# Attention scores of two key heads as two 64-row tiles of the matmul array instead of 96 or 100 zero-padded rows

## The chip, the cores and the metric

The kernel runs on one core of a Trainium2 chip. The metric is device time in microseconds (us) of one execution; the time before is the median of three executions. One further execution was recorded by the hardware profiler, and every duration below comes from it. Engine names are those of the profile: PE is the matmul array, PEld its weight loads, DVE the vector engine, ACT the scalar engine, POOL the general engine, SP the queue from which this kernel issues its DMAs.

## The reference, cut to what matters

Two layers run one after the other on `x` of 2 x 512 tokens x 512 channels, each with a modulated layer norm, an attention block and a feed-forward block. Layer 0 is a gated chunked linear attention with 32 heads of 128, then a ternary-weight feed-forward. Layer 1 is a softmax attention with small heads (which the change touches), then a mixer of four streams whose 4x4 matrices are balanced by 50 Sinkhorn iterations per token.

```python
# layer 1 attention: 32 query heads, 8 key heads, 16 channels each; called with x of 2 x 512 x 512
xq = (x @ wq + bq).reshape(B, S, H, D)
xk = (x @ wk + bk).reshape(B, S, KV, D)
xv = (x @ wv + bv).reshape(B, S, KV, D)
q = _rope(xq, cos, sin)
k = _rope(xk, cos, sin)
k = jnp.repeat(k, REP, axis=2)          # REP = 4 query heads per key head
v = jnp.repeat(xv, REP, axis=2)
scores = jnp.einsum('bqhd,bkhd->bhqk', q, k) / jnp.sqrt(jnp.float32(D))
probs = jax.nn.softmax(scores.astype(jnp.float32), axis=-1)
out = jnp.einsum('bhqk,bkhd->bqhd', probs, v).reshape(B, S, E)
```

## The kernel before, in words

**Number format of the scores.** A score is a sum over 16 channels, which the kernel computes with 48 rows of the array: queries and keys are each split into a high and a low part, the queries stand in memory as (high, high, low) and the keys as (high, low, high), 3 x 16 = 48 rows per key head (`q_dram`, `k_dram`, written by `rope_halves`, L665). The exponent needs the row's maximum subtracted, and that too is done by the matmul: two further rows hold the negated maximum, again as a high and a low part, against key rows that are one.

**A step and its tiles.** A step (`order`, L1185) is one batch `b`, one half of the 512 queries (256) and one of four pairs `t` of key heads; there are 16. For a step, `key_rows` and `keys1` (L786, L793) fill two tiles `ks`, one for each key head s of the pair, [128, 512]: head 0 has its keys in rows 0 to 47 and zeros in 48 to 95, head 1 zeros in 0 to 47 and its keys in rows 48 to 95, and rows 96 to 99 hold the ones and zeros that pick the right maxima. `queries1` (L800) fills two tiles `qs`, one for each pair `rp` of query heads, [128, 2, 256], with the queries of head 0 in rows 0 to 47 and of head 1 in rows 48 to 95. So every score matmul contracts 96 rows (`KS`) for the maxima or 100 (`KM`) for the weights, of which 48 or 50 bring something. The zeros come from constants (`c_keys1`) that `layer1_keys` (L741) loads, copies on ACT and spreads by DMA over six tiles `ks`; three sets of key tiles rotate over the steps (`key_tile`).

**Pieces.** A step is worked in eight pieces, so there are 128. Piece k of a step does in `maxima` (L834) two score matmuls of 512 columns (L843), 128 queries against 512 keys, and a DVE maximum over each (L847). After each fourth piece the eight columns of maxima are split into high and low parts (L853, L854), transposed on PE (L857), copied by ACT (L862) and sent by a DMA into rows 96 to 99 of `qs` (L863). `weigh` (L865) does for a piece four score matmuls of 256 columns with the operands swapped (keys stationary, L877), and ACT takes the exponential of two at a time (L68, tile `pt`). After four pieces (a quad) `outputs` (L887) multiplies by the values: 32 matmuls in column tiles of 32 (L897), then ACT copies (L909), and `finish` (L911) transposes (L918), divides and adds to the residual.

**Order.** A loop over 64 units of layer 0 issues the first pieces from unit 53 on (`FIRST`, `PER`, `HOLD`), so layer 1's attention for batch 0 runs beside layer 0's end for batch 1; the rest follows in the loop of `piece` (L1219), which calls `maxima`, then, 10 pieces behind (`LAG`), `weigh`, then `outputs` and `finish`, and steps the generators `streams` (the mixer) by two steps per piece (`aside`). The tile framework orders the instructions within each engine's queue from its own estimate of their times, with the priorities and order-only dependencies (`anchor`, `behind`, L897's "one run of column tiles") that the kernel adds. PSUM tiles `s1` (L842) and `s2` (L874) are asked for with three buffers each (`S1`, `S2`). After the last piece the last two mixer groups finish alone.

Of the kernel before, what the change touches and what calls it, by code (L numbers as in the profile page):

```python
# [9 lines left out]
FP = mybir.dt.float32  # L10
FR = mybir.dt.float32r
W1 = 2
PT, OUT = 16, 1
S1, S2, MT, OT, OP = 3, 3, 2, 2, 2
# [18 lines left out]
AF = mybir.ActivationFunctionType  # L33
ALU = mybir.AluOpType
AX = mybir.AxisListType
PSUM = bass.MemoryType.PSUM

P = 128
B, L, HID = 2, 512, 512
NC = L // P  # L40
# [13 lines left out]
def tile_adaln(ctx: ExitStack, tc: tile.TileContext, a: dict, out: bass.AP):  # L54
    nc = tc.nc
# [6 lines left out]
    psp = ctx.enter_context(tc.tile_pool(name="ps", bufs=2, space=PSUM))  # L62
# [4 lines left out]
    def act(o, i, func, **kw):  # L67
        ins = nc.scalar.activation(o, i, func, **kw)  # L68
        tc.add_manual_dep(
            ins.ins, table.ins.name,  # L70
            mybir.DependencyInfo(mybir.DependencyClass.NoSync, mybir.DependencyReason.DATA),
            reason="the activation table",
        )
        return ins.ins
# [43 lines left out]
    anchor = {}  # L118
# [33 lines left out]
    def temp(shape, dt, name, bufs=2):  # L152
        return wk.tile(shape, dt, name=name, bufs=bufs)

    def bank(shape, name, bufs=2):
        return psp.tile(shape, FP, name=name, bufs=bufs)
# [42 lines left out]
    def raw_tile(load):  # L199
        raw = raws.tile([P, KC * P], FP, name="raw")  # L200
        nc.sync.dma_start(out=raw, in_=load)
        return raw
# [153 lines left out]
    ps = bank([64, HID], "mps")  # L356
# [285 lines left out]
    k_dram = [dram.tile([KV1, 48, L], FP, name=f"k_dram{b}") for b in range(B)]  # L642
# [88 lines left out]

    Q = L // 2
    NQ = Q // P
    KS, KM = 96, 100
    ksd = {}

    holder = {}

    def layer1_keys(js=(0, 1)):  # L741
        for s in range(2):
            empty = temp([P, L], FR, "hi1")
            nc.scalar.copy(empty, raw_tile(a["c_keys1"][s]))
            for j in js:
                ksd[j, s] = temp([P, L], FR, f"ks{j}{s}")
                nc.sync.dma_start(out=ksd[j, s].bitcast(FP), in_=empty.bitcast(FP))

    steps = [(g, b) for g in range(KV0 - AHEAD) for b in range(B)]
    steps += [(g, b) for b in range(B) for g in range(KV0 - AHEAD, KV0)]  # L750
# [33 lines left out]
    def key_tile(i):  # L784
        return i % 2 if i < TWO else (i - TWO + 2) % 3

    def key_rows(i):
        j = key_tile(i)
        if j == 2 and (2, 0) not in ksd:
            layer1_keys((2,))  # L790
        return [ksd[j, s] for s in range(2)]

    def keys1(i):  # L793
        b, t = order[i]["b"], order[i]["t"]
        order[i]["ks"] = key_rows(i)
        holder[key_tile(i)] = i
        for s in range(2):
            nc.sync.dma_start(out=order[i]["ks"][s].bitcast(FP)[48 * s:48 * s + 48], in_=k_dram[b][2 * t + s])

    def queries1(i):  # L800

        b, half, t = (order[i][n] for n in ("b", "half", "t"))
        assert l1c["there", b]
        pair = []
        for rp in range(2):
            qs = temp([P, 2, Q], FR, "qs", QS)
            for s in range(2):
                h = 8 * t + 4 * s + 2 * rp
                nc.sync.dma_start(
                    out=qs.bitcast(FP)[48 * s:48 * s + 48],  # L810
                    in_=q_dram[b][h:h + 2, :, half * Q:half * Q + Q].rearrange("r k q -> k r q"),
                )
            pair.append(qs)
        return pair
# [18 lines left out]

    def maxima(st, k):  # L834

        assert holder[key_tile(st["i"])] == st["i"]
        rp, j = divmod(k, 4)
        s, i = divmod(j, 2)
        if j == 0:
            st["m"] = small.tile([P, NQ * 2, 2], FP, name="m")  # L840
        for qt in range(NQ):
            ps = psp.tile([P, L], FP, name="s1", bufs=S1)  # L842
            anchor["pe"] = nc.tensor.matmul(  # L843
                ps, lhsT=st["qs"][rp][0:KS, i, qt * P:(qt + 1) * P], rhs=st["ks"][s][0:KS],
                start=True, stop=True,
            ).ins
            anchor["dve"] = nc.vector.tensor_reduce(  # L847
                st["m"][:, 2 * qt + s, i:i + 1], ps, AX.X, ALU.max, negate=True
            ).ins
        if j == 3:  # L850
            m2 = small.tile([P, NQ * 2, 2, 2], FR, name="m2")
            hi, lo = m2[:, :, 0], m2[:, :, 1]
            nc.vector.tensor_copy(hi, st["m"])  # L853
            nc.vector.tensor_tensor(lo, st["m"], hi.bitcast(FP), ALU.subtract)  # L854
            mt = psp.tile([8, Q], FP, name="mt", bufs=MT)
            for qt in range(NQ):
                nc.tensor.transpose(  # L857
                    mt[:, qt * P:(qt + 1) * P],
                    m2[:, 2 * qt:2 * qt + 2].bitcast(FP).rearrange("p a b c -> p (a b c)"), ident,
                )  # L860
            mm = temp([8, L], FR, "mm")[:, 0:Q]
            nc.scalar.copy(mm, mt)  # L862
            anchor["sp"] = nc.sync.dma_start(out=st["qs"][rp].bitcast(FP)[96:100], in_=mm.bitcast(FP)).ins  # L863

    def weigh(st, k):  # L865

        assert holder[key_tile(st["i"])] == st["i"]
        rp, r = divmod(k, 4)
        kp, s = divmod(r, 2)
        if r == 0:  # L870
            quads.append({"st": st, "rp": rp, "pt": {}})
        qd = quads[-1]
        for i in range(2):
            ps = psp.tile([P, 2, Q], FP, name="s2", bufs=S2)  # L874
            for j in range(2):
                kt = 2 * kp + j
                nc.tensor.matmul(  # L877
                    ps[:, j, :], lhsT=st["ks"][s][0:KM, kt * P:(kt + 1) * P], rhs=st["qs"][rp][0:KM, i, :],
                    start=True, stop=True,
                )  # L880
            p = wts.tile([P, 2, Q], FP, name="pt", bufs=PT)
            anchor["act"] = qd["last"] = act(p, ps, AF.Exp, scale=0.25)
            qd["pt"][2 * s + i, kp] = p

    quads = []

    def outputs(j):  # L887


        qd = quads[j]  # L890
        st = qd["st"]
        op = psp.tile([P, 2, Q], FP, name="op", bufs=OP)[:, 0, :]
        first = None
        with tc.high_priority(UPO):
            for kt in range(NC):
                for r in (3, 0, 1, 2):
                    mm = nc.tensor.matmul(  # L897
                        op[32 * r:32 * r + 32, :], lhsT=va[st["b"]][kt // 2][:, kt % 2, 2 * st["t"] + r // 2, :],
                        rhs=qd["pt"][r, kt // 2][:, kt % 2, :], start=kt == 0, stop=kt == NC - 1,
                    ).ins  # L900
                    if first is None:
                        first = mm
                        last_pt = qd["last"]
                        for m in (anchor["pe"], last_pt):
                            tc.add_manual_dep(mm, m.name, order_only, reason="behind the scores at hand")
                    else:
                        tc.add_manual_dep(mm, first.name, order_only, reason="one run of column tiles")
        qd["os"] = temp([P, L], FP, "os")[:, 0:Q]
        nc.scalar.copy(qd["os"], op)  # L909
# [57 lines left out]
    def streams(b, c0, n, last, ways):  # L967
# [217 lines left out]
    order = [  # L1185
        {"b": b, "half": half, "t": t} for b in range(B) for half in range(2) for t in range(4)
    ]
# [11 lines left out]
    def load_step(i):  # L1199
        if i < len(order):  # L1200
            o = order[i]
            o["i"] = i
            o["qs"] = queries1(i)
# [4 lines left out]
    def begin():  # L1208
        with behind():
            row_tiles(0, (GA,))  # L1210
        load_step(0)
        keys1(0)
        values1(0)
# [5 lines left out]
    def piece():  # L1219
        p = at[0]  # L1220
        at[0] += 1
        if p == 0:
            begin()
        i, k = divmod(p, 8)
        if k == 0 and i < len(order):
            load_step(i + 1)
        if p < n_pieces:
            maxima(order[i], k)
        if wt[0] <= p - slack(p):
            weighed()  # L1230
        if k == 4 and i + 1 < len(order):
            keys1(i + 1)
        with tc.high_priority(UP):
            if p >= HOLD and p % POP == 0 and virtual:
                tail(virtual.pop(0))
        aside(2)
# [64 lines left out]
    for n, u in enumerate(units):  # L1301
        g, b, c = u["at"]
        s = n // NC
# [127 lines left out]
```

## Time and profile before

| | |
|---|---|
| median of 3 executions | 1407.75 us (1398.83 to 1408.99) |
| the profiled execution: its own time | 1409.56 us |
| its span, first to last instruction | 1407.8 us |
| mean granted clock of PE | 0.944 |
| busy: PE, DVE, ACT, POOL | 1247.3, 1164.4, 825.1, 787.2 us |
| L843, the maxima's score matmuls | 256, first at 898.3 us, last at 1261.4 us |
| L877, the weights' score matmuls | 512, from 925.1 to 1275.6 us |
| L847, DVE maxima | 256, mean 673 ns |
| L68 on `pt`, ACT exponentials | 256, mean 601 ns |
| last matmul of layer 0's projections (L233) | ends at 1116.6 us |

How to read it: the busy time of an engine is the union of its instructions' records. A matmul's record is longer than the time for which it holds the array, since the next one starts before its end; what it holds is read from the distance of two starts. A wait is put down to the instruction that came last. The granted clock of PE is the share of its full clock, recorded in steps of about 3.41 us, each at 1.0 or at 0.5.

### The profile page before, as it was taken

To read this page: it belongs to the slowest core of one execution; us is meant where nothing else is said; L and a number is where in the kernel's file an instruction comes from. 1 tells how busy PE (TensorE), PEld (TensorE's weight loads), DVE (VectorE), ACT (ScalarE), POOL (GpSimd) and SP (SyncE) were. 2 spreads that over 40 slices of the span, in tenths; PEclk is the share of its full clock that TensorE was granted. 3 is DMA by queue.
4 is the path that set the end of the run, shared out by engine and by line. 5 is a ranking of instruction groups with operands and counts; after the bars stand their busy time and mean duration, and the time that the engine had idled before them with its cause. 6 is when DMAs were issued, how large, how long until landed. Compare 5 with 4: busy or idle time off the path is not lost. (4 is left out here: it accounts for less than half of the span.)

```text
span 1407.8 us, 23038 instructions
## 1 busy us (share of the span) xinstructions
PE 1247.3 (89%) x7128; PEld 990.5 (70%) x7128; DVE 1164.4 (83%) x3171; ACT 825.1 (59%) x2333; POOL 787.2 (56%) x1180
## 2 busy tenths in 40 slices
PE   6979999999999999999988998899998899994117
PEld 3767888788788778888876777677776667762116
DVE  7998668687677687787999977788699879888998
ACT  5456576476476466666665655567567467653226
POOL 4363274365264367577777757644243644657854
PEclk9999999999999999999999999999999899986568
DMA  7121241231131233224333327623212331100001
GB/s 241 36 70 43 87 124 39 68 106 53 53 118 56 94 117 111 81 79 128 120 106 90 98 70 233 179 66 97 65 42 94 101 92 48 59 2 1 1 15 46
DMA packets 95378, 117.14 MB, mean 83 GB/s; under 512 B 10828, under 2 KB 50508, under 8 KB 95256
## 3 DMA queue, kind: packets, MB, share of 16 engines
q1 hardware_dynamic: 95256, 115.67, 27.6%
q8 instruction: 57, 0.93, 0.3%
q14 instruction: 65, 0.53, 0.1%
HBM read 102.11 MB, written 10.64 MB: 80 GB/s over the span
## 5 line engine op out<-in xcount | busy, mean ns | idle before, releaser
L847 DVE TENSOR_REDUCE m<-s 128x1 f32<-128x512 f32 x256 | 166.6, 673 | 21.8 <-PE s L843 21.5
L68 ACT ACTIVATE pt<-s 128x512 f32<-128x512 f32 x256 | 137.4, 601 | 33.1 <-PE s L877 31.5
L448 POOL TENSOR_TENSOR q<-xcos,rot 128x512 f32<-128x512 f32 x64 | 92.8, 1450 | 56.5 <-DVE xcos L446 52.5
L68 ACT ACTIVATE sg<-sg 128x512 f32<-128x512 f32 x128 | 80.7, 632 | 64.5 <-DVE sg L479 62.5
L496 POOL TENSOR_SCALAR_AFFINE_SELECT dec<-gb 128x512 f32<-128x512 f32 x64 | 48.3, 755 | 121.2 <-DMA gb<-g_dram 65.4
L843 PE MATMUL s<-ks,qs 96*128 96x512 f32 x256 | 104.9, 442 | 11.5 <-DVE m L847 7.6
L877 PE MATMUL s<-qs,ks 100*128 100x256 f32 x512 | 104.4, 309 | 10.2 <-DMA qs<-mm 6.8
L233 PE MATMUL pps<-hh,wq_h 128*128 128x512 f32 x256 | 103.3, 403 | 7.1 <-ACT vT L767 3.4
L877 PEld LDWEIGHTS s<-qs,ks 100*128 100x128 f32 x512 | 82.7, 199 | 32.8 <-issue 7.9
L68 ACT ACTIVATE dec<-dec,room 128x128 f32<-128x128 f32 x256 | 83.0, 398 | 34.8 <-POOL dec L496 34.6
L233 PE MATMUL ops<-wo_h,zh 128*128 128x512 f32 x256 | 102.2, 399 | 1.2 <-ACT zh L571 1.0
L233 PE MATMUL gps<-wg_h,hh 128*128 128x512 f32 x256 | 101.3, 398 | 1.5 <-ACT wg_h L210 1.2
L233 PE MATMUL ops<-wo_h,zl 128*128 128x512 f32 x256 | 101.5, 396 | 0.7 <-DVE zl L572 0.7
L233 PE MATMUL pps<-hl,wq_h 128*128 128x512 f32 x256 | 101.8, 398 | 0.0
L233 PE MATMUL pps<-hh,wq_l 128*128 128x512 f32 x256 | 101.5, 397 | 0.0
L233 PE MATMUL gps<-wg_l,hh 128*128 128x512 f32 x256 | 101.1, 395 | 0.0
L233 PE MATMUL ops<-wo_l,zh 128*128 128x512 f32 x256 | 100.6, 393 | 0.0
L233 PE MATMUL gps<-wg_h,hl 128*128 128x512 f32 x256 | 100.6, 393 | 0.0
L516 POOL TENSOR_TENSOR gb<-gb,q 128x512 f32<-128x512 f32 x48 | 62.3, 1299 | 60.3 <-ACT gb L68 46.7
L549 PE MATMUL yps<-v,dec 128*128 128x128 f32 x512 | 93.4, 278 | 2.7 <-DVE xcos L446 1.4
L555 ACT ACTIVATE z<-yps 128x128 f32<-128x128 f32 x256 | 67.5, 278 | 41.1 <-PE yps L551 30.5
L559 DVE SCALAR_TENSOR_TENSOR z<-yps,ss,sg 128x128 f32<-128x128 f32 x256 | 72.0, 340 | 22.5 <-ACT ss L68 22.3
(321 smaller groups left out, 3984.4 us busy)
## 6 DMA issues: line engine op xcount, KB each, us to landing
gb<-g_dram SPq DMA_DIRECT2D x64, 256.0 KB
raw<-in_wq SPq DMA_DIRECT2D x56, 256.0 KB
raw<-in_wg SPq DMA_DIRECT2D x48, 256.0 KB
raw<-in_wo SPq DMA_DIRECT2D x48, 256.0 KB
raw<-in_wmod SPq DMA_DIRECT2D x40, 256.0 KB
qs<-q_dram SPq DMA_DIRECT2D x64, 96.0 KB
q_dram<-hi SPq DMA_DIRECT2D x16, 256.0 KB
raw<-in_wk SPq DMA_DIRECT2D x14, 256.0 KB
```

The lines of the kernel that those rows point to most:

```text
L68: ins = nc.scalar.activation(o, i, func, **kw)
L233: nc.tensor.matmul(ps, lhsT=l, rhs=r, start=i == 0, stop=i == n - 1)
L448: nc.gpsimd.tensor_tensor(dst, sp(xc_), sp(rot), ALU.add)
L496: anchor["pool"] = nc.gpsimd.affine_select(out=dec, in_=gb, pattern=[[0, REP0], [1, P]], compare_op=ALU.is_ge, fill=-1e30, base=0, channel ...
L516: nc.gpsimd.tensor_tensor(gb, gb, q[:, c], ALU.mult)
L549: nc.tensor.matmul(yps[:, h, :], lhsT=u["pr"][:, h, :], rhs=u["v"][:, c, :], start=True, stop=not c)
L555: nc.scalar.activation(z[:, h, :], yps[:, h, :], AF.Square, accum_out=ss[:, h:h + 1])
L559: nc.vector.scalar_tensor_tensor(z[:, h, :], yps[:, h, :], ss[:, h:h + 1], sg[:, h * P:(h + 1) * P], ALU.mult, ALU.mult)
L843: anchor["pe"] = nc.tensor.matmul(ps, lhsT=st["qs"][rp][0:KS, i, qt * P:(qt + 1) * P], rhs=st["ks"][s][0:KS], start=True, stop=True,).ins
L847: anchor["dve"] = nc.vector.tensor_reduce(st["m"][:, 2 * qt + s, i:i + 1], ps, AX.X, ALU.max, negate=True).ins
L877: nc.tensor.matmul(ps[:, j, :], lhsT=st["ks"][s][0:KM, kt * P:(kt + 1) * P], rhs=st["qs"][rp][0:KM, i, :], start=True, stop=True,)
```

## The change

Each key head's scores become a matmul of their own 48 rows (`KS`) or 50 (`KM`), head 0 on rows 0 to 63 of the array and head 1 on rows 64 to 127. One tile `ks` then holds both heads of a step, so there are three in place of six, and only two rows of ones per head are set up, by small DMAs from one loaded constant. The two matmuls of a pair, s = 0 and s = 1, are issued one right after the other, into two PSUM tiles that are both taken before the first of them. A piece of `maxima` is now one 128-query tile of both heads in place of two tiles of one; a piece of `weigh` is 128 keys of both heads with the 512 columns of both query heads in one matmul, in place of two matmuls of 256 for each head. The DMA of the maxima becomes two, one for each head.

```diff
-    KS, KM = 96, 100
+    KS, KM = 48, 50
...
     def layer1_keys(js=(0, 1)):
-        for s in range(2):
-            empty = temp([P, L], FR, "hi1")
-            nc.scalar.copy(empty, raw_tile(a["c_keys1"][s]))
-            for j in js:
-                ksd[j, s] = temp([P, L], FR, f"ks{j}{s}")
-                nc.sync.dma_start(out=ksd[j, s].bitcast(FP), in_=empty.bitcast(FP))
+        empty = temp([P, L], FR, "hi1")
+        nc.scalar.copy(empty, raw_tile(a["c_keys1"][0]))
+        for j in js:
+            ksd[j] = temp([P, L], FR, f"ks{j}")
+            for s in range(2):
+                nc.sync.dma_start(
+                    out=ksd[j].bitcast(FP)[64 * s + KS:64 * s + KM], in_=empty.bitcast(FP)[96:98]
+                )
...
-            nc.sync.dma_start(out=order[i]["ks"][s].bitcast(FP)[48 * s:48 * s + 48], in_=k_dram[b][2 * t + s])
+            nc.sync.dma_start(out=order[i]["ks"].bitcast(FP)[64 * s:64 * s + KS], in_=k_dram[b][2 * t + s])
...
-                    out=qs.bitcast(FP)[48 * s:48 * s + 48],
+                    out=qs.bitcast(FP)[64 * s:64 * s + KS],
...
         rp, j = divmod(k, 4)
-        s, i = divmod(j, 2)
+        i, qt = divmod(j, 2)
         if j == 0:
             st["m"] = small.tile([P, NQ * 2, 2], FP, name="m")
-        for qt in range(NQ):
-            ps = psp.tile([P, L], FP, name="s1", bufs=S1)
+        pss = [psp.tile([P, L], FP, name="s1", bufs=S1) for s in range(2)]
+        for s in range(2):
             anchor["pe"] = nc.tensor.matmul(
-                ps, lhsT=st["qs"][rp][0:KS, i, qt * P:(qt + 1) * P], rhs=st["ks"][s][0:KS],
-                start=True, stop=True,
+                pss[s], lhsT=st["qs"][rp][64 * s:64 * s + KS, i, qt * P:(qt + 1) * P],
+                rhs=st["ks"][64 * s:64 * s + KS], start=True, stop=True,
             ).ins
+        for s in range(2):
             anchor["dve"] = nc.vector.tensor_reduce(
-                st["m"][:, 2 * qt + s, i:i + 1], ps, AX.X, ALU.max, negate=True
+                st["m"][:, 2 * qt + s, i:i + 1], pss[s], AX.X, ALU.max, negate=True
             ).ins
...
-            anchor["sp"] = nc.sync.dma_start(out=st["qs"][rp].bitcast(FP)[96:100], in_=mm.bitcast(FP)).ins
+            for s in range(2):
+                anchor["sp"] = nc.sync.dma_start(
+                    out=st["qs"][rp].bitcast(FP)[64 * s + KS:64 * s + KM], in_=mm.bitcast(FP)[4 * s:4 * s + 4]
+                ).ins
...
-        for i in range(2):
-            ps = psp.tile([P, 2, Q], FP, name="s2", bufs=S2)
-            for j in range(2):
-                kt = 2 * kp + j
-                nc.tensor.matmul(
-                    ps[:, j, :], lhsT=st["ks"][s][0:KM, kt * P:(kt + 1) * P], rhs=st["qs"][rp][0:KM, i, :],
-                    start=True, stop=True,
-                )
+        pss = [psp.tile([P, 2, Q], FP, name="s2", bufs=S2) for s in range(2)]
+        for s in range(2):
+            nc.tensor.matmul(
+                pss[s], lhsT=st["ks"][64 * s:64 * s + KM, kt * P:(kt + 1) * P], rhs=st["qs"][rp][64 * s:64 * s + KM],
+                start=True, stop=True,
+            )
+        for s in range(2):
             p = wts.tile([P, 2, Q], FP, name="pt", bufs=PT)
-            anchor["act"] = qd["last"] = act(p, ps, AF.Exp, scale=0.25)
-            qd["pt"][2 * s + i, kp] = p
+            anchor["act"] = qd["last"] = act(p, pss[s], AF.Exp, scale=0.25)
+            qd["pt"][s, kt] = p
...
-                        rhs=qd["pt"][r, kt // 2][:, kt % 2, :], start=kt == 0, stop=kt == NC - 1,
+                        rhs=qd["pt"][r // 2, kt][:, r % 2, :], start=kt == 0, stop=kt == NC - 1,
```

## The prediction, made before the changed kernel ran

> **What bounds the kernel now.** First the page: busy shares and the granted clock of PE in 40 slices.
>
> ```profile
> PE 1247.3 (89%) x7128; PEld 990.5 (70%) x7128; DVE 1164.4 (83%) x3171; ACT 825.1 (59%) x2333; POOL 787.2 (56%) x1180
> ...
> PEclk9999999999999999999999999999999899986568
> ```
>
> The changed matmuls run from 898 to 1276 us, so the second view is the windows of that part: PE, PEld, DVE, ACT, POOL busy, then clock, DMA share, GB/s.
>
> ```profile
> 895.00:1000.00 105.00, 96.89 (x558) 76.86 (x557) 90.35 (x189) 69.68 (x192) 48.45 (x43) 0.97 0.33 92
> 1000.00:1135.00 135.00, 125.70 (x889) 93.68 (x887) 124.48 (x323) 83.81 (x220) 62.37 (x86) 0.95 0.25 79
> 1135.00:1280.00 145.00, 135.07 (x1163) 94.33 (x1163) 119.22 (x445) 95.90 (x230) 79.83 (x316) 0.93 0.14 40
> 1280.00:1408.00 128.00, 42.27 (x258) 40.00 (x258) 115.87 (x759) 43.55 (x156) 84.15 (x318) 0.63 0.05 17
> ```
>
> PE leads, DVE is close behind; after 1280 only the mixer's DVE and POOL work is left, which the change doesn't touch. I call 895 to 1135 the mixed stage (layer 0 still runs) and 1135 to 1280 the attention stage. Third, the groups and the waits of the attention stage.
>
> ```profile
> L847 DVE TENSOR_REDUCE m<-s 128x1 f32<-128x512 f32 x124 | 81.4, 673 | 18.9 <-PE s L843 18.7
> L68 ACT ACTIVATE pt<-s 128x512 f32<-128x512 f32 x144 | 76.2, 600 | 20.5 <-PE s L877 19.8
> L877 PE MATMUL s<-qs,ks 100*128 100x256 f32 x288 | 58.6, 310 | 7.5 <-DMA qs<-mm 6.8 <-ACT pt L68 0.6
> L843 PE MATMUL s<-ks,qs 96*128 96x512 f32 x123 | 50.3, 436 | 1.2 <-DVE m L847 1.2
> ...
> L897 PE MATMUL op<-pt,va 128*32 128x256 f32 x608 | 42.4, 423 | 0.5 <-ACT pt L68 0.5
> ```
>
> ```profile
> ACT os L909 <- PE op L897: 25.4, 17, 3.2
> ...
> DVE m L847 <- PE s L843: 18.7, 19, 3.1
> ...
> PE s L877 <- DMA qs<-mm: 6.8, 8, 2.1
> ```
>
> The others wait for PE; DVE could give back 18.7 us at most. Fourth, PE's timeline, since records overlap and only starts tell what a matmul holds.
>
> ```profile
> 1164.80 0.40 PE L843 MATMUL s<-ks,qs 96*128 96x512 f32 x1
> 1165.04 0.40 PE L877 MATMUL s<-qs,ks 100*128 100x256 f32 x2
> ...
> 1166.67 0.39 PE L843 MATMUL s<-ks,qs 96*128 96x512 f32 x1
> 1166.99 1.94 PE L897 MATMUL op<-pt,va 128*32 128x256 f32 x32
> 1168.86 0.50 PE L843 MATMUL s<-ks,qs 96*128 96x512 f32 x1
> ```
>
> 512 columns hold PE 0.237 us, 256 half of it. Into the column tiles it is 0.32 (0.09 more), and out of them about as much: 0.31 from the last start of `op`. One `op` of 32 matmuls takes 1.87 us by the chain of waits, and 3.45 where the clock is halved (1136.7). Last, the clock, by windows of its own 3.41 us steps; here I show the busy time of all engines, clock last but two.
>
> ```profile
> 1201.67:1205.08 3.41, 2.48 (x15) 1.72 (x14) 3.29 (x9) 1.24 (x4) 1.27 (x6) 1.00 0.22 60
> ...
> 1235.80:1239.22 3.42, 3.42 (x14) 2.74 (x12) 2.96 (x10) 3.07 (x9) 2.10 (x8) 0.50 0.00 0
> 1239.22:1242.63 3.41, 3.41 (x33) 1.39 (x32) 1.38 (x8) 0.57 (x2) 1.78 (x9) 0.50 0.00 0
> ...
> 1252.87:1256.28 3.41, 2.76 (x14) 1.79 (x13) 3.41 (x13) 1.84 (x5) 1.31 (x6) 1.00 0.01 2
> ```
>
> The step after 1252.87 is at half, though PE was busy 2.76 us; the one after 1201.67 stays full with 2.48; 1235.80 is all busy, with scores, and the next is still at half. What orders these is columns weighted by rows: counting each matmul's columns times its share of 128 rows (384 for a maxima matmul, 200 for a weight one, 512 for each four of `op`, whose plain float32 takes two passes), by start times, the steps hold 3,130 (stays full), 3,050 (stays half) and 2,900 (falls). I take 3,090 as the bound. It falls in 5 of the 42 steps of the attention stage.
>
> **The change, part by part.** *Key tiles.* Three loads of 256 KB, three ACT copies of 618 ns and ten DMAs of 256 KB go; ten DMAs of 4 KB come. They lie at 842 to 890, beside a DMA share of 0.77 (850 to 900); ACT waits there 10.7 us for weights (`wg_h`), PE only 1.2 for ACT. I take -1, bounds -4 and 0.
>
> *Scores, mixed stage.* 133 maxima matmuls and 224 weight ones start there: 133 x 0.237 + 224 x 0.118 = 58 us of PE. In full pairs half goes, 29. Two row tiles side by side are not in this trace: a pair takes between 0.237 us (both at once) and 0.474 (one after the other). The nearest rows are `op`'s column tiles, four at once in 1.87/8 = 0.23, so I take the former where nothing else parts a pair. The weight loads allow it, if only just: L983's matmuls of 24 columns, each with a load of 128, start 0.112 us apart, and two loads are 0.224. PE is busy 222.6 of 240 and DVE 214.8, so what was PE's ends up behind DVE: DVE's idle time there is 25 us, of which `rot`, `m` and `xres` name PE for 3.6 + 2.8 + 1.3 = 7.7. I take -8; bounds -25 (all idle time of DVE) and +4 (no pairs, and about 40 changes between scores and layer 0's projections at 0.09).
>
> *Scores, attention stage, with the clock.* PE's array time at full clock by starts: 123 x 0.237 + 288 x 0.118 = 63.2 of scores; 19 `op` with both switches at 2.05 = 39.0; 144 transposes and small matmuls at 0.11 = 15.8; 118 us. At half clock it is about 228. With 12% of steps at half, 1/T = 0.88/118 + 0.12/228, T = 125: the stage's 145 is this and 20 of waits. After: scores 31.6 in full pairs; `op` as before; 54 visits of transposes and small matmuls, which now change the tiling too, 54 x 0.18 = 9.7 (bounded by nothing and by `op`'s rows, taken at the latter, the nearest). Sum 96.1 at full clock, 174 at half. But the weighted columns of a score fall from 384 and 2 x 200 to 192 and 200 per 512: per quad from 6,270 + 4,096 (`op`) + 512 to 3,140 + 4,096 + 512. Steps without `op` hold 1.7 pieces x 784, under the bound; a step needs about 1,900 columns, 0.87 us, of `op`. A quad takes 7.6 us, 2.24 steps, and `op` of 1.87 us fills that much of 1.05 steps. So 1.05/2.24 = 47% of the steps are followed by full clock, 53% by half: T = 126 in full pairs, and 139 if 30% of pairs run one after the other (9.5 more at full clock, 19 at half). I take the middle, 132.5: +8. Bounds: -22 (PE out of the way: DVE's 18.7 and 3.8 of waits for PE) and +44 (no pairs at all, rival three).
>
> By the page "TensorE: Matmul & The Clock Gate" (HAM oscillation) of the Trainium skill the clock falls where PE idles for over some 3 us. The rows above say otherwise, as PE's longest wait near a fall is 2.1 us. By the page the share at half wouldn't rise, and the sum would be that of rival one.
>
> *Second DMA of the maxima.* SP issues 32 more at 0.636 us. Queued behind are the loads of the next step's `qs` and `ks`, a step ahead, so hidden. But head 1's rows land 0.64 us later, and the L877 matmul of head 1 waits, with all of PE's queue behind it. Eight such waits exist in the attention stage: 8 x 0.64 = 5; half of them I take as given back by slack, +3, bounds 0 and +11 (17 quads).
>
> *DVE, ACT, PSUM.* The same 256 maxima of 673 ns and 256 exponentials of 601, in another order: nothing. Pairs take two of three buffers at once; where DVE is late, the second matmul waits 0.65 us for a bank and the pair falls apart. That is in the 30% above.
>
> The Trainium skill's page "TensorEngine Tiling (Array Packing)" (Key Properties) speaks against the change: changing the tiling mode drains PE. It gives no price; with a whole record's tail, 0.40 - 0.24 = 0.16 us, as an estimate, the 108 changes of the attention stage cost 7 us more than at 0.09, and the sum would be 1417.
>
> **Sum.** 1409.56 - 1 - 8 + 8 + 3 = 1411.6. The profiled execution is 1.8 above the median, so 1410.
>
> **Rivals.** *One, faster: the clock holds.* For it: `op` is full-array work in every quad. Against: the count by steps. With 12% at half T is 101.5, so DVE becomes the bound; of the 22 us that it waits for PE I take 15, and -10 in the mixed stage: 1409.6 - 1.8 - 15 - 10 - 1 = 1382.
>
> *Two, slower: the clock gate.* In the attention stage scores alone never reach the bound, `op` falls into halved steps (3.45 for 1.87), and half the pairs come apart as DVE releases banks one at a time. At 70% of steps at half and half the pairs: 111.9 full, 205.6 half, T = 164, +39, less some 12 of today's 20 us of waits, +27; mixed stage -6, DMA +5, tiles -1: 1433. It decides from about 63% of the steps at half: with 30% unpaired T is then 148, 23 more, less some 3 of waits, and the sum is 1% above the time before. For it: every step without `op` falls; against: batch 0's pieces run beside full-array work.
>
> *Three: the pairs don't run together at all.* Then PE saves nothing, switches come on top and the rows still count half: 127.7 and 237, T = 169, +44 less 12; mixed +4, DMA +3, tiles -1: 1446. Against: `op`'s tiles overlap four at a time.
>
> **How the numbers follow.** Forecast 0.42, own range 1398 to 1422; rival one 0.25, two 0.25, three 0.08. A measurement of this kernel tells about 1%, 14 us, from no change. So faster 0.25, same 0.42, slower 0.33. Low 1380 leaves a third of rival one out (0.08), high 1440 rival three and a little of two (0.12).
>
> **What would show it.** Right: L843 and L877 with 48 and 50 rows, two starts within some 0.03 us and the next pair 0.24 later; clock in 1135 to 1280 near 0.75 (0.93 now); `op` at 3.45 in about half the quads; DVE's wait for L843 as large as now; the mixed stage about 8 us shorter. The clock still at 0.9 means rival one; starts of a pair 0.24 apart, rival three. A reordering of the queues by the framework that moves other stages by over 10 us makes the sum wrong for a reason outside it.

## The result, and the profile after

In executions that took turns on one chip the changed kernel took 1453.36 us (median of 4) and the kernel before 1406.32 (median of 4): a ratio of 1.0331, with a 95% interval of 1.0273 to 1.0389. It is slower by 46.6 us, beyond the range (1380 to 1440) and beyond every rival. The profiled execution took 1453.35 us, with a span of 1451.6.

The page of the changed kernel, busy time of PE and the other engines, and the granted clock in 40 slices:

```profile
PE 1291.2 (89%) x6872; PEld 958.4 (66%) x6872; DVE 1174.9 (81%) x3171; ACT 826.0 (57%) x2330; POOL 784.5 (54%) x1180
...
PEclk9999999999999999999999998998988998777665
```

PE has 256 matmuls fewer, is as busy as before in share, and in time 44 us longer. The clock's digits are under 9 in seven of the slices from the 25th to the 36th, where before two were; the last four are low in both kernels, with the mixer alone.

Now the windows, with each kernel's own stage bounds: the mixed stage ends with the last projection of layer 0 (1116.6 us before, 1140.7 after), the attention stage with the last `op` (1278.5 and 1326.1). The last three columns are clock, DMA share, GB/s. The kernel before, then the changed one:

```profile
895.00:1117.00 222.00, 209.50 (x1357) 160.67 (x1355) 198.97 (x472) 141.98 (x387) 98.02 (x103) 0.97 0.27 78
1117.00:1279.00 162.00, 147.76 (x1250) 104.05 (x1250) 134.16 (x477) 107.08 (x254) 91.70 (x336) 0.92 0.19 55
```

```profile
895.00:1141.00 246.00, 231.69 (x1237) 151.33 (x1237) 196.27 (x473) 141.85 (x386) 97.41 (x110) 0.89 0.23 71
1141.00:1326.00 185.00, 167.44 (x1126) 79.94 (x1124) 151.00 (x582) 110.52 (x259) 115.15 (x464) 0.84 0.15 47
```

Each stage lost 24 us. What follows the last `op` takes 125.5 us against 129.3, so nothing was lost there. Twice (1 - clock) times the length of a window is its time at half clock; by the clock's own records the mixed stage has 54.9 us of it (before 13.7) and the attention stage 58.8 (before 27.3).

The groups of the attention stage after: busy time, mean of one, idle time before them and what ended it.

```profile
L852 DVE TENSOR_REDUCE m<-s 128x1 f32<-128x512 f32 x138 | 89.5, 666 | 17.6 <-PE s L847 13.2 <-PE s L882 4.1
L68 ACT ACTIVATE pt<-s 128x512 f32<-128x512 f32 x160 | 85.8, 601 | 34.1 <-PE s L882 29.8 <-PE s L847 3.4
L882 PE MATMUL s<-qs,ks 50*128 50x512 f32 x160 | 63.1, 506 | 8.8 <-DMA qs<-mm 5.1 <-DVE m L852 2.7 <-ACT pt L68 0.9
L903 PE MATMUL op<-pt,va 128*32 128x256 f32 x672 | 60.1, 496 | 3.5 <-ACT pt L68 3.5
L847 PE MATMUL s<-ks,qs 48*128 48x512 f32 x138 | 55.7, 496 | 5.0 <-DVE m L852 4.3
```

```profile
ACT os L915 <- PE op L903: 21.1, 14, 3.0
...
DVE m L852 <- PE s L847: 13.2, 12, 4.4
```

DVE and ACT work as fast as before (666 and 601 ns) and still wait for PE, DVE as long as before (17.6 us, 18.9 in the shorter stage before), ACT longer (34.1 against 20.5). So PE still bounds, though it has half as many scores to pay for where pairs run together.

PE's timeline of the changed kernel shows why. A record with x2 or more joins neighbours.

```profile
957.16 0.60 PE L567 MATMUL ztp<-room,z 128*128 128x128 f32 x4
957.69 0.50 PE L847 MATMUL s<-ks,qs 48*128 48x512 f32 x2
958.03 0.40 PE L882 MATMUL s<-qs,ks 50*128 50x512 f32 x2
958.27 0.40 PE L847 MATMUL s<-ks,qs 48*128 48x512 f32 x1
958.51 0.40 PE L882 MATMUL s<-qs,ks 50*128 50x512 f32 x1
...
1216.02 0.73 PE L847 MATMUL s<-ks,qs 48*128 48x512 f32 x1 [0.45 <-DVE m L852]
1216.68 3.31 PE L903 MATMUL op<-pt,va 128*32 128x256 f32 x32
```

Its weight loads at the same place:

```profile
957.69 0.18 PEld L847 LDWEIGHTS s<-ks,qs 48*128 48x128 f32 x2 [0.17 <-issue]
957.80 0.19 PEld L882 LDWEIGHTS s<-qs,ks 50*128 50x128 f32 x2
```

And a load of the kernel before, whose matmul, the first line of the prediction's fourth view, starts at 1164.80:

```profile
1164.69 0.19 PEld L843 LDWEIGHTS s<-ks,qs 96*128 96x128 f32 x1
```

Three things are to be seen. Two score matmuls do start together (957.69, x2; the second 4 ns after the first), and the next two 0.34 us later, not 0.24. The loads show what goes with it: behind other work the pair's loads start with their matmuls, at 957.69, and the next pair's 0.11 us later; in the trace of before the load ran 0.11 us ahead of its matmul. This is no single case: of the 146 score matmuls that follow full-array work or column tiles in the changed kernel's trace, 144 start within 30 ns of their load, while before, behind full-array work, a load is 0.116 us ahead (median). And then single score matmuls follow each other at 0.24 us (958.27, 958.51), as without tiling: by starts within 60 ns, only 129 times did two scores run together, and 254 ran alone.

### The profile page after: what moved, and what is told of

Read it like the earlier page. It is cut to its first block, busy times and chain, and to the rows that moved or that the text cites. A ratio compares the mean times of both kernels' runs of the same rounds, so it can differ in the third digit from the quotient of the medians.

```text
span 1451.6 us, 22557 instructions
## 1 busy us (share of the span) xinstructions
PE 1291.2 (89%) x6872; PEld 958.4 (66%) x6872; DVE 1174.9 (81%) x3171; ACT 826.0 (57%) x2330; POOL 784.5 (54%) x1180
## 4 chain that ended last, share of the span: by engine, by line
PE 47%; DVE 25%; POOL 11%; issue 9%; ACT 4%; DMA 4%; SPq 0%; POOLq 0%; ACTq 0%; DVEq 0%
PE pps L233 11%; PE ops L233 8%; PE gps L233 7%; PE op L903 4%; DVE m L852 3%; PE yps L549 3%; PE s L882 2%; PE sps L233 2%; PE s L847 2%; POOL q L448 2%; PE yps L551 2%; DVE ql L455 2%; PE mps L272 1%; POOL wq_l L211 1%; PE cps L233 1%
## 5 line engine op out<-in xcount | busy, mean ns | idle before, releaser
L847 PE MATMUL s<-ks,qs 48*128 48x512 f32 x256 | 102.7, 499 | 10.2 <-DVE m L852 9.1
L882 PE MATMUL s<-qs,ks 50*128 50x512 f32 x256 | 98.9, 503 | 11.6 <-DMA qs<-mm 5.6
L1167 PE MATMUL mix<-h,dg 128*128 128x128 f32 x192 | 35.4, 337 | 72.0 <-ACT dg L1166 71.9
L523 POOL TENSOR_TENSOR xw<-v,room 128x512 f32<-128x512 f32 x48 | 55.2, 1164 | 77.1 <-ACT v L463 73.6
L903 PE MATMUL op<-pt,va 128*32 128x256 f32 x1024 | 89.6, 495 | 3.7 <-ACT pt L68 3.7
```

The lines of the kernel that those rows point to most:

```text
L523: nc.gpsimd.tensor_tensor(xw, u["v"][:, c, :].unsqueeze(1).to_broadcast(sh4), wdc[:, c, r0:r0 + REP0].unsqueeze(2).to_broadcast(sh4), ALU. ...
L847: anchor["pe"] = nc.tensor.matmul(pss[s], lhsT=st["qs"][rp][64 * s:64 * s + KS, i, qt * P:(qt + 1) * P], rhs=st["ks"][64 * s:64 * s + KS], ...
L882: nc.tensor.matmul(pss[s], lhsT=st["ks"][64 * s:64 * s + KM, kt * P:(kt + 1) * P], rhs=st["qs"][rp][64 * s:64 * s + KM], start=True, stop= ...
L903: mm = nc.tensor.matmul(op[32 * r:32 * r + 32, :], lhsT=va[st["b"]][kt // 2][:, kt % 2, 2 * st["t"] + r // 2, :], rhs=qd["pt"][r // 2, kt] ...
L1167: nc.tensor.matmul(mps[:, i], lhsT=dg[:, j], rhs=hv[:, j] if j < NS else yb[:, c], start=j == 0, stop=j == NS)
```

## The experiments

Each ratio is to the kernel before, run in turn on the same chip, with its 95% interval. Three theories were held against each other. *Torn pairs:* pairs that come apart lose the overlap. *Changes:* each change of tile shape (full array, two 64-row tiles, four column tiles) costs PE time; in PE's queue between the first and the last score there are 318 of them, before 118. *Clock:* fewer rows counted, so more time at half. Theories of weight loads and of the order of the pieces are in the first expectations.

**A stream of matmuls alone.** No attention: matmuls of the shapes in question, back to back. `pair` is two 48-row tiles of 512 columns, `tile_` one of them, `rows` an untiled matmul, `turns` two transposes.

```diff
+    for k in range(72):
+        pair(k)
...
+    for k in range(64):
+        tile_(0, k)
...
+    for k in range(24):
+        for j in range(2):
+            rows(96, 2 * k + j)
+        turns(k)
+    for k in range(24):
+        pair(2 * k)
+        pair(2 * k + 1)
+        turns(k)
```

> A stream of matmuls alone, in a fixed order, without anything that PE would wait for (no attention, no layers; the output is the input x). Stretches: 72 pairs of 48-row tiles from a cold start, 64 matmuls of 96 rows, 72 pairs again, 64 of 128 rows, 64 matmuls of 48 rows all in the lower tile, 64 of 128 rows, 40 pairs of 64 rows, 64 of 128 rows, and then 24 times each: two 96-row matmuls and two transposes; two pairs and two transposes; two 96-row matmuls and eight column-tile matmuls; two pairs and eight of them; one 48-row matmul and two transposes. Theory torn pairs (the tiles work as the prediction had it, but the pairs were taken apart in the queue): a pair every 0.24 us at full clock. Theory weight loads (a tile's weights can't be loaded ahead while the tile is in use, so each pair shows a load): a pair every 0.33 us, as the changed kernel's trace has it between pairs, and a lone 48-row stream in one tile 0.33 as well, against 0.23 for 96 and 128 rows. Theory clock (rows are counted): 48-row matmuls in one tile fall to half clock within two steps of 3.4 us though PE is never idle; pairs of 48 rows that start at half stay there, pairs that start at full stay at full.

The timeline of PE in this stream, L42 being untiled matmuls, L45 the 48-row tiles, L55 transposes:

```profile
39.05 16.64 PE L45 MATMUL b<-yr,xr 48*128 48x512 f32 x144
...
70.37 22.84 PE L45 MATMUL b<-yr,xr 48*128 48x512 f32 x64
...
137.27 0.38 PE L55 MATMUL b<-ident,x 128*128 128x128 f32 x2
137.41 0.71 PE L42 MATMUL b<-yr,xr 96*128 96x512 f32 x2
137.96 0.38 PE L55 MATMUL b<-ident,x 128*128 128x128 f32 x2
...
152.64 0.44 PE L55 MATMUL b<-ident,x 128*128 128x128 f32 x2
153.01 0.73 PE L45 MATMUL b<-yr,xr 48*128 48x512 f32 x4
153.67 0.44 PE L55 MATMUL b<-ident,x 128*128 128x128 f32 x2
```

A dense stream of pairs goes at 0.227 us a pair, as the prediction assumed. The first one, from a cold start, began at 0.427 us a pair, half clock, and went to full by itself after 6.3 us. The clock theory had it stay at half: at that pace the pairs count 3,072 weighted columns in a step of 3.41 us, just under the bound of 3,090, so this expectation missed. But two untiled matmuls and two transposes repeat every 0.69 us (137.27 to 137.96), two pairs and two transposes every 1.03 (152.64 to 153.67): a visit of full-array work costs 0.345 us, two changes of 0.17. And the 64 lone 48-row matmuls took 22.8 us, though each holds PE for 0.227 at full clock: from 76.0 to 96.5 us the clock was at half, with PE never idle. So in a dense stream a pair is no slower in itself, its weight loads don't slow it, and lone tiles lose twice, in overlap and in clock.

**The order of the pieces, untiled.** Everything of the change but the tiles: 96 and 100 rows, the new pieces, with two DMAs of the maxima and with one.

```diff
-    KS, KM = 48, 50
+    KS, KM = 96, 100
...
-                pss[s], lhsT=st["qs"][rp][64 * s:64 * s + KS, i, qt * P:(qt + 1) * P],
-                rhs=st["ks"][64 * s:64 * s + KS], start=True, stop=True,
+                pss[s], lhsT=st["qs"][rp][0:KS, i, qt * P:(qt + 1) * P], rhs=st["ks"][s][0:KS],
+                start=True, stop=True,
```

> The kernel before with all of the change but the tiles: the matmuls of both heads issued one after the other into two banks, the weights as one matmul of 512 columns for both query heads, the maxima sent by two DMAs, but 96 and 100 zero-padded rows as before. Theory torn pairs, and theory clock: the tiles cost the time, so this is within 1% of before, 1395 to 1420. Theory order (the new order and the second DMA upset the queues): 1435 to 1455.

> As order_two, but with the one DMA of the maxima of before. All theories but order: within 1% of before. Theory order: less than order_two by what the second DMA costs; if that is the 0.64 us of each of the 17 quads of the attention stage, 11 us less.

Two DMAs: 1415.45 us, 1.0057 (1.0029 to 1.0086). One: 1413.6 us, 1.0053 (1.0032 to 1.0073). The new order costs about 0.5%, some 7.5 us, and the second DMA nothing that can be measured. The tiling, with the rows that it leaves out, is the rest, 2.8% or 39 us.

**Pairs kept together.** The first matmul of a pair also waits for what frees the second's bank, and for both DMAs.

```diff
+            if s == 0:
+                together(anchor["pe"], "m")
...
+            if s == 0:
+                together(mm, "pt", st["landed", rp])
```

> The changed kernel, in which the first matmul of a pair also waits for what its second one waits for (the reader that frees the second's bank, the second DMA of the maxima), so that both are ready together; in the queue of PE 225 of 256 pairs then stand next to each other, against 78. Theory torn pairs: most of the loss comes back, 1405 to 1425. Theory weight loads: pairs still take 0.33 us, some comes back, 1425 to 1440. Theory clock: the array is used no more than before, so more steps fall to half, 1445 or more.

1460.23 us, 1.0372 (1.0310 to 1.0433), no better, though now 202 times two scores run together. The windows of this kernel, mixed and attention stage:

```profile
895.00:1113.00 218.00, 204.30 (x1140) 132.52 (x1139) 183.15 (x423) 131.74 (x361) 90.72 (x94) 0.93 0.24 73
1113.00:1346.00 233.00, 197.52 (x1283) 96.66 (x1282) 186.01 (x713) 135.63 (x328) 137.63 (x568) 0.74 0.14 41
```

The mixed stage is as short as before (1113 against 1117), and the attention stage 71 us longer, with 119.5 us at half clock. The theory of torn pairs falls as the cause of the loss: with the pairs mended the mixed stage's time comes back, and the attention stage loses more, with 92 us more at half clock than before. What the added waits cost by themselves was not taken apart.

**What the clock counts, and what a change costs.** A second stream, with lone tiles of 64 rows, of 56, and of 64 of which 32 are zero, with transposes done as 64-row tiles, and with columns alone.

```diff
+            for s in range(2):
+                put(nc.tensor.transpose(
+                    b[4 + 2 * s + j][:, 0:64], x[64 * s:64 * s + 64, w(k + j)], ident[64 * s:64 * s + 64, 64 * s:64 * s + 64],
+                ).ins)
```

> A stream of matmuls alone, whose output is x and not the reference's. It asks what the clock counts and what a change between tilings costs. Theory rows (the clock follows columns times rows, bound about 3,090 per step of 3.41 us): a lone tile of 64 rows, one 512-column matmul every 0.227 us, counts 3,845 and stays full; one of 56 rows counts 3,364 and stays full; the 48 rows of the stream before counted 2,884 and fell. If zeros count as rows, the stream of 64 rows of which 32 are zero stays full; if only data counts it falls. Rival (a lone tile falls because half the array is idle, whatever its rows): all three fall to half within two steps. Theory changes (every change of tile shape costs 0.17 us): the transposes as pairs of 64-row tiles between pairs of scores lose the 0.345 us that a visit cost, a period near 0.68 in place of 1.03; columns alone take 1.66 - 0.454 - 0.345 = 0.86 us a period; two 128-row matmuls of 512 columns after two pairs cost 0.345 more than after two 96-row ones, 1.25 against 0.91. Rival (the transposes are slow to start because of their small loads): all of these keep the difference, 0 or 0.345 alike.

PE's timeline of this stream (L51 and L79 lone tiles, then L51 pairs, L74 the tiled transposes):

```profile
21.41 14.82 PE L51 MATMUL b<-yr,xr 64*128 64x512 f32 x64
...
50.90 14.82 PE L51 MATMUL b<-yr,xr 56*128 56x512 f32 x64
...
80.38 14.82 PE L79 MATMUL b<-yz,xz 64*128 64x512 f32 x64
...
110.42 0.28 PE L74 MATMUL b<-ident,x 64*128 64x64 f32 x4
110.52 0.71 PE L51 MATMUL b<-yr,xr 48*128 48x512 f32 x4
111.06 0.29 PE L74 MATMUL b<-ident,x 64*128 64x64 f32 x4
```

64 matmuls take 14.8 us in all three, so the clock stays full; at 48 rows they took 22.8. The bound lies between 48 and 56 rows here, as the count of columns times rows said (2,884 and 3,364 about a bound of 3,090), and rows of zeros count. The transposes as 64-row tiles repeat every 0.64 us (110.42 to 111.06) where the full ones took 1.03. Part of this is that the tiled ones are shorter, 0.13 us a period by themselves against 0.22; beside them and two pairs (0.454) about 0.05 us is left of the 0.345. So without a change of shape the cost is nearly gone, and it isn't the small loads. Two 128-row matmuls of 512 columns after two pairs took 0.42 more than their own time, a little over the 0.345 expected. Columns alone took 0.86 a period, as expected, so the change to column tiles costs the same, from either shape.

**More rows for the tiled kernel.** Each score matmul contracts all 64 rows of its tile, the added ones zero. In the variant with pairs kept, five buffers of `qs` stand for six.

```diff
-                pss[s], lhsT=st["qs"][rp][64 * s:64 * s + KS, i, qt * P:(qt + 1) * P],
-                rhs=st["ks"][64 * s:64 * s + KS], start=True, stop=True,
+                pss[s], lhsT=st["qs"][rp][64 * s:64 * s + 64, i, qt * P:(qt + 1) * P],
+                rhs=st["ks"][64 * s:64 * s + 64], start=True, stop=True,
...
-                pss[s], lhsT=st["ks"][64 * s:64 * s + KM, kt * P:(kt + 1) * P], rhs=st["qs"][rp][64 * s:64 * s + KM],
+                pss[s], lhsT=st["ks"][64 * s:64 * s + 64, kt * P:(kt + 1) * P], rhs=st["qs"][rp][64 * s:64 * s + 64],
```

> The changed kernel with every score matmul contracting the whole 64 rows of its tile, the added rows zero in queries and keys (64 small DMAs more; the result is the same). The matmuls take the same time; only the rows that the clock may count rise, from 96 or 100 to 128 a pair. Theory clock (rows count, and half clock is a large part of the loss): the 114 us at half between 895 us and the end of op fall to about 85, and the time from 1453 to about 1440. Theory changes (the loss is the 0.345 us per visit; the clock only follows the waits): the share at half and the time stay, 1453 within 5.

> The variant in which both matmuls of a pair wait for the same (pairs stay together; 1460, with 119.5 us at half clock in the attention stage), with 64 rows in each tile, the added ones zero, and five buffers of queries in place of six for room. Theory clock: its 150 us at half between 895 us and the end of op fall to about 110 and the time to about 1442. Theory changes: both stay, 1460 within 6. The lost buffer can only cost; a time above 1466 is that.

1426.88 us, 1.0114 (1.0073 to 1.0155), and with pairs kept 1426.95, 1.0126 (1.0090 to 1.0163): rows of zeros, which bring nothing to the sum, take 2.2% and 2.5% off, more than expected. Time at half falls from 114 to 75 us and from 150 to 81. The windows of the first:

```profile
895.00:1127.00 232.00, 219.02 (x1224) 143.51 (x1222) 196.36 (x466) 137.88 (x375) 90.72 (x100) 0.93 0.24 75
1127.00:1301.00 174.00, 157.55 (x1134) 77.35 (x1133) 144.05 (x543) 112.24 (x263) 106.07 (x409) 0.88 0.19 57
```

The zeros come by DMAs, which the framework orders among the others, so a control keeps the DMAs and takes the rows away.

```diff
-                pss[s], lhsT=st["qs"][rp][64 * s:64 * s + 64, i, qt * P:(qt + 1) * P],
-                rhs=st["ks"][64 * s:64 * s + 64], start=True, stop=True,
+                pss[s], lhsT=st["qs"][rp][64 * s:64 * s + KS, i, qt * P:(qt + 1) * P],
+                rhs=st["ks"][64 * s:64 * s + KS], start=True, stop=True,
```

> The control for the tiled kernel with 64 rows (1.0114 of the time before): the same 64 additional DMAs of zeros, but the score matmuls still contract 48 and 50 rows as in the changed kernel (1.0331). PE's queue has 287 changes of tile shape, against 294 with 64 rows and 318 in the changed kernel. Theory clock (the rows make the difference): between 1.025 and 1.033 of the time before, with 100 us or more at half clock between 895 us and the end of op. Rival (the DMAs shift the queues, and the order of the queues made the difference): 1.012 to 1.016, near 75 us at half.

1442.91 us, 1.0253 (1.0225 to 1.0282). Its windows:

```profile
895.00:1134.00 239.00, 227.46 (x1274) 149.34 (x1274) 200.28 (x469) 140.99 (x383) 92.65 (x102) 0.90 0.23 72
1134.00:1320.00 186.00, 173.49 (x1092) 83.33 (x1088) 139.38 (x512) 108.92 (x254) 99.69 (x382) 0.75 0.17 53
```

It spends 138 us at half, and the mean clock of its four executions is 0.914, that of the four with 64 rows 0.934. So the rows are worth 1.0253 - 1.0114, 1.4% or 19.5 us. The other 0.8% goes with the queues' new order (287 changes of shape in place of 318), though the two intervals touch and the size of it is not sure.

**More rows for the untiled kernels.** 128 rows in every score matmul, for the control with the new order and one DMA, and for the kernel before.

```diff
+            nc.sync.dma_start(
+                out=qs.bitcast(FP)[96:P], in_=ksd[0, 0].bitcast(FP)[48:80].rearrange("p (k q) -> p k q", k=2)
+            )
...
-                ps, lhsT=st["qs"][rp][0:KS, i, qt * P:(qt + 1) * P], rhs=st["ks"][s][0:KS],
+                ps, lhsT=st["qs"][rp][:, i, qt * P:(qt + 1) * P], rhs=st["ks"][s],
```

> The untiled control with the new order of the pieces and one DMA of the maxima (1413.6, of which 37.6 us at half clock between 895 us and the end of op), with 128 rows in every score matmul, the added ones zero (one DMA more for each tile of queries). It counts as many rows for two 512-column matmuls as the tiled kernel with 64 rows counts for two pairs, or more; what differs from that kernel (1426.9) is the tiling alone: fewer changes of tile shape (some 128 against 294), but no pairs. Theory changes (0.345 us per visit cost more than the pairs save): well below 1426.9, 1403 to 1412. Rival (with the clock settled the tiling costs nothing, and what is left of the loss comes from the order): 1420 or more. Theory clock for itself: below 1413.6 by 3 to 8 us, with 25 us or less at half.

> The kernel before with 128 rows in every score matmul, the added rows zero, the zeros sent by one DMA ahead of the loads of each tile of queries. Theory clock: the 41 us at half between 895 us and the end of op fall to 25 or less and the time by 3 to 8 us, to about 1401. If the clock of the kernel before only follows waits: 1406 within 4.

With the new order 1404.93 us, 0.9997 (0.9980 to 1.0015), 0.6% under its control; time at half goes from 37.6 to 17.9 us. The tiled kernel with 64 rows, 1.0114, is 1.2% or some 16 us slower than this, as the theory of changes expected: the untiled one counts as many rows or more, so the tiling still costs that much, its 75 us at half clock included. The kernel before with 128 rows takes 1396.21 us, 0.9925 (0.9902 to 0.9948), more of a gain than the 3 to 8 us expected: it beats both kernels of this study. The windows of the latter, where the mixed stage never falls to half:

```profile
895.00:1104.00 209.00, 201.53 (x1343) 153.33 (x1341) 194.38 (x466) 138.93 (x383) 94.36 (x100) 1.00 0.28 82
1104.00:1260.00 156.00, 141.79 (x1249) 99.93 (x1249) 132.84 (x471) 105.75 (x253) 88.99 (x328) 0.97 0.21 62
```

The control of this one keeps the zeros' DMAs and contracts 96 and 100 rows again:

```diff
-                ps, lhsT=st["qs"][rp][:, i, qt * P:(qt + 1) * P], rhs=st["ks"][s],
+                ps, lhsT=st["qs"][rp][0:KS, i, qt * P:(qt + 1) * P], rhs=st["ks"][s][0:KS],
```

> The same control for the kernel before with 128 rows (0.9925 of the time before, 10 us at half clock between 895 us and the end of op): its 32 additional DMAs of zeros, with 96 and 100 rows contracted as before. Theory clock: 0.998 to 1.004, some 40 us at half. Rival (the DMAs shift the queues for the better): 0.990 to 0.995.

1406.77 us, 1.0013 (0.9998 to 1.0028). So the DMAs win nothing and the rows 0.9%, about 12 us. But the control's own profile has only 20.7 us at half, not 40, and the same time as the kernel before; 10 us less at half are worth 5 at most. That profiled execution (mean clock 0.949) is at the upper end of its kind: the mean of the control's twelve executions is 0.946, as of the kernel before, and that of the six with 128 rows 0.950. Over the whole span this is 153 us at half against 139, and 14 us less are worth 7 of the 12 at most. That the rows win here is shown; that they win it all through the clock is not.

**Changes without pairs.** In the untiled control with one DMA the maxima's matmul of head 0 contracts 64 rows, a lone tile whose rows from 48 on are zero, and that of head 1 128 rows. The rows counted stay the same, nothing runs together, and PE's queue has 355 changes of shape in place of 128; or 229, with lone tiles in every second pair.

```diff
-                pss[s], lhsT=st["qs"][rp][0:KS, i, qt * P:(qt + 1) * P], rhs=st["ks"][s][0:KS],
+                pss[s], lhsT=st["qs"][rp][0:(64, P)[s], i, qt * P:(qt + 1) * P], rhs=st["ks"][s][0:(64, P)[s]],
```

> What the changes of tile shape cost inside the kernel, with nothing gained for them: the untiled control with the new order and one DMA (1413.6), in which the maxima's matmul of head 0 contracts 64 rows (a lone 64-row tile, its rows 48 to 63 zero) and that of head 1 contracts 128 (full array), 96 rows on the mean as in the control, the weights' matmuls as there. No two matmuls run together; the rows that the clock counts are the same; in PE's queue the changes of tile shape rise from 128 to 355. Theory changes: 227 times 0.17 = 39 us of PE, of which waits hide up to a third: 1440 to 1453. Rival (the drain hides behind the tail of the record, and what tiling costs is something else): 1414 within 6.

> The same with lone tiles in only every second pair of the maxima (64 of 128); the changes of tile shape in PE's queue are 229. Theory changes: 101 times 0.17 = 17 us of PE: 1425 to 1431, about half of what the other shows. Rival: 1414 within 6.

PE's timeline of the first, a lone tile between full-array matmuls:

```profile
1163.29 0.40 PE L878 MATMUL s<-qs,ks 100*128 100x512 f32 x1
1163.62 0.49 PE L846 MATMUL s<-ks,qs 64*128 64x512 f32 x1
1164.04 0.50 PE L878 MATMUL s<-qs,ks 100*128 100x512 f32 x1
```

0.33 us into the tile and 0.42 out of it, where 512 columns hold PE 0.237. Both variants also send the 32 DMAs of zeros, which their control lacks; in the kernel before such DMAs made 1.0013. The times are 1435.48 us, 1.0186 (1.0155 to 1.0217), and 1424.23, 1.0116 (1.0080 to 1.0153). Against the control's 1.0053 that is 1.33% or 18.7 us for 227 changes, and 0.63% or 8.9 us for 101: 0.08 to 0.09 us each, in proportion. That the changes cost time is shown, but only half of the 0.17 us of PE reaches the end time, where I expected two thirds or more; the first run misses its lower end by 5 us, the second by 1. Time at half hardly moves (42.0 and 31.5 us; control 37.6).

## Why the prediction was wrong

Of the 46.6 us, as an estimate, the order of the pieces is some 7.5 (measured in a control), the rows that the tiles left out some 19.5 (what 64 rows in place of 48 or 50 in each tile give back, by the control), and the 190 changes of shape above the 128 of that control some 16, at 0.085 (the price that lone tiles show there). These sum to 43. Two more terms of opposite sign were not measured apart: what the pairs save, and what is left at half clock even with 64 rows (75 us, where the untiled control with 128 rows has 17.9; a pair of 64 rows counts half as much for each score). By the sum they nearly cancel. But the terms were measured in different kernels, and that they add up is not shown: of the 0.8% (11 us) that goes with the queues' new order in the control with the zeros' DMAs, 31 changes fewer explain 2.6 us, and the rest is in no term.

- *Scores, mixed stage, -8:* the step that failed worst. The stage is 24 us longer; some 6 of these are lost by 904 us, since the framework put the first scores 23 us earlier (874.9) and the clock was at half from 885.0 to 898.7. I counted the rows for the attention stage only and let layer 0's work hold the clock here; it fell to half for 54.9 us, before 13.7. And the changes stood only in the bound (+4, some 40 at 0.09); in the queue they rise from 50 to 170.
- *The pace of a pair, 0.237:* right in a dense stream (0.227) and in the kernel at best (0.232), wrong behind a change of shape (0.333 to 0.344 us from a pair to the next score in 42 of 48 cases at full clock). The nearest row, four column tiles, was measured inside a run of 32 alike. I weighed the loads' length against the pair's and missed that behind a change of shape they don't start early.
- *Pairs apart, 30%:* 129 of 256 ran together, so half came apart. In PE's queue only 78 pairs stand next to each other: the framework sorted the rest apart. I had thought of late banks only, and named reordering just as something that could upset the sum. Yet with 202 together the kernel is no faster.
- *Switches, 0.18 a visit:* 0.345 in PE time in the stream. `op`'s rows gave only the part by which starts move apart; and I counted 54 visits of the attention stage alone. The Trainium skill's page "TensorEngine Tiling (Array Packing)" (Key Properties), which says that a change of mode drains PE, agrees with the stream, where each change costs PE time: the 0.16 us that I had estimated for a change stands beside 0.17 measured.
- *Attention stage, clock, +8:* the stage lost 24 us. That the scores alone fall to half clock was right, its size not. Half clock took 32% of the stage, not 53%, so more half clock is not what the term lacked. The new changes (54 visits, 108) were not too few, since in PE's queue they rise there from 68 to 148, but each was priced at half of the stream's 0.17 us; and half of all pairs came apart, not 30% at most. What each adds in this stage no run took apart. Where the pairs are kept together, as I had reckoned them, half clock takes 119.5 of 233 us, 51%. `op`, given as 3.45 us in about half the quads, is stretched in 14 of 21. The clock in the window 1135 to 1280 was 0.85, between the 0.75 that I gave and 0.93.
- *The order of the pieces, nothing:* it costs some 7.5 us, by a control in which nothing is tiled. *Second DMA, +3:* nothing that shows. *Key tiles, -1:* no run took them apart.
- *The rivals.* One falls, since the clock did not hold. Three falls: pairs start 4 ns apart. Two named both things that went wrong, half clock and pairs apart, but put them in the attention stage alone, and its mixed stage still gained 6 us.

By the page "TensorE: Matmul & The Clock Gate" (HAM oscillation) of the Trainium skill, weighed in the prediction, idle time of PE lowers the clock. The stream of lone 48-row tiles shows that no idle time is needed: it fell 5.6 us after it began (70.4 to 76.0) with no gap, and the same stream with 56 rows did not fall.

The count orders the kernels but not every step: some steps of the changed kernel with 2,400 to 2,700 weighted columns stayed full, and in the kernel before the step after 1194.84, at half with some 2,990, was followed by full clock. In the streams lone tiles at 2,884 fell and pairs at 3,072 rose, so 3,090 is a little high as well as too sharp. (What the count and the kernel's description call 32 matmuls of `op` are the profile's records; the source issues 16.) What else the clock follows stays open.

## What to carry to other kernels

Tiles of the array paid here only where they filled a whole run, in the stream (0.227 us for a pair, as for one matmul): before tiling, count the changes of shape in PE's own queue, not in the source, at up to 0.17 us of PE each, of which about half reached the end time here. Where the profile's clock sags while PE is busy, look at the rows that its matmuls contract before looking for idle time: zero rows cost a matmul nothing (0.227 us with 96 or 128 rows, or with 64 of which 32 are zero) and here won 0.75% for the kernel that was already there, while the change, which took rows away, lost some 19.5 us with them. And price a rule in every stage where the changed work runs, not only where it is densest.

## What the runs showed of the hardware

- A continuous stream of matmuls of 48 rows in one tile falls to half clock within 5.6 us; 56 rows, 64, and 64 with 32 of zeros stay full over 14.8 us, and so do pairs of 48, which even return from half to full.
- A change among full array, 64-row tiles and 32-column tiles costs 0.17 us of PE on the mean of the way in and out (0.345 a visit; 0.42 for visits of 512 columns). Behind it the next weight load starts with its matmul instead of 0.11 us ahead; that this is the whole cost is not shown.
- Transposes as two 64-row tiles beside 48-row pairs cost next to no change, about 0.05 us a visit: a period of 0.64 us in place of 1.03.
